# Cross-attention on one core: the loop's maxima are added onto the scores by accumulating transfers instead of GpSimd subtractions

## The chip, the cores and the metric

The kernel runs on one core of a Trainium2 chip. A core has TensorE (PE, matmuls; its weight loads are shown apart as PEld), VectorE (DVE), ScalarE (ACT), GpSimd (POOL) and SyncE (SP), and sixteen DMA engines that move data between HBM and the on-chip memory SBUF and within SBUF. The metric is the time of one execution on the device in microseconds.

## What is computed

For each of 16 batch items, 1024 query rows of 512 features attend to 64 context rows, in 16 heads of 32 features. Both inputs go through a layer norm whose scale and shift come from a condition vector. In the reference (cut to what matters):

```python
xq  = _ada_ln(x_q, t_vec, Wss_q, bss_q)
xkv = _ada_ln(x_kv, t_vec, Wss_kv, bss_kv)
q = (xq @ Wq + bq).reshape(B, Lq, nh, dh)
kv = (xkv @ Wkv + bkv).reshape(B, Lkv, 2, nh, dh)
scores = jnp.einsum('bqhd,bkhd->bhqk', q, k) / jnp.sqrt(jnp.float32(dh))
attn = jax.nn.softmax(scores, axis=-1)
out = jnp.einsum('bhqk,bkhd->bqhd', attn, v).reshape(B, Lq, H)
return x_q + (out @ Wp + bp)
```

All is float32. The change touches the softmax: the subtraction of the maximum of the scores ahead of the exponential.

## The kernel before the change

The queries are handled in 32 blocks of 512 rows (`NB = 32`). The engines' programs are written out by hand: the order of the calls in the Python text is the order in each engine's queue. A prologue computes keys and values for all batch items and starts the first blocks, a loop `for i in range(3, NB - 2)` (27 iterations) holds the steady state, and an end part finishes blocks 30 and 31. One iteration works on several blocks at once: the scores and the softmax of block `i`, the mix with the values and the output of `a = i - 1`, the rest of the output of `b = i - 2`, the query products of `n = i + 1`, the features of `f = i + 2`, and norm and transposes of later blocks.

The products of the queries and of the output use a scheme of seven products of half-size blocks (`query_product(n, k)`, `product(a, k)`), with sums of blocks made by GpSimd (`feature_sums`, `feature_quarters`, `row_sum`). Products add up in PSUM banks; `output_seed(a)` (L1039) is a ScalarE copy of one bank into another, onto which `product(a, 2)` then adds.

The softmax of block `i` goes this way. The 64 context rows are two halves, z = 0 and 1. `score_products(i, z)` (L738) makes the scores in PSUM, 32 keys of four heads on the partitions. VectorE takes the maximum of each 32 by transposing in the reduction (`maximum`, L755), ScalarE copies the scores to SBUF (`copied`, L764) as `s_tiles[i, z]`, 128 x 2048 values or 1 MB. `maxima(i)` joins the maxima of both halves on VectorE (L775, a tile `m` of 128 x 64) and spreads them back over the keys by a transpose (L784) into `mb`, again 128 x 2048. `subtract(i, zs)` (L797) subtracts `mb` from `s` in place, on GpSimd. `weights(i, z)` (L808) is ScalarE's exponential, in place for z = 0 and into a tile `p` for z = 1. Then `total(i)` adds both halves on GpSimd (L858), `swapped(i)` and `again` bring the halves into the form that the mix reads, and `row_total`, `inverse_rows` (L878, L881, L883, by way of a small tensor `ltd` in HBM and back as `vr`) and `spread_rows` (L891) make the inverse of the sums, by which `divided` (L915) multiplies the mix's results.

SyncE issues the transfers: loads of the block `x` (L119, 1 MB) and of the residual `r` (L126, 1 MB), the output (L1118, two halves of 512 KB), the moves `xt<-ht` (L382, sixteen of 64 KB for a block) that finish the transposition of the features, and the small ones of the inverse.

In the loop `subtract(i, zs=(0,))` and `subtract(i, zs=(1,))` are apart in the text, but no other GpSimd work lies between them. On ScalarE `weights(i, 0)`, `weights(i, 1)` and `output_seed(a)` follow one another, behind `scale_features(f, (3,))` (L442) and `biased(a, 2)` (L1031).

Of the kernel before, what the change touches and what calls it, by code (L numbers as in the profile page):

```python
# [11 lines left out]
ALU = mybir.AluOpType  # L12
# [8 lines left out]
def cross_attention_block(  # L21
# [18 lines left out]
    nc = tc.nc  # L40
# [10 lines left out]
    NB = B * BPB  # L51
# [675 lines left out]
    s_tiles, m_tiles = {}, {}  # L727
# [45 lines left out]
    def both(dst, src, op):  # L773

        nc.vector.tensor_reduce(dst, src.rearrange("p z r j -> p (r j) z"), AX.X, op)  # L775

    def spread(i, src, name, other=False):
        if other:

            t = qpool.tile([P, 4, NC, NT * 32], F32, tag="xt", name=name)  # L780
            t = t.rearrange("p g c n -> p (g c n)")
        else:
            t = rpool.tile([P, HPC * TB], F32, tag="spread", name=name)
        nc.vector.transpose(t, src.unsqueeze(2).to_broadcast([P, HPC * NJ, 32]))  # L784
        return t.rearrange("p (r q) -> p r q", r=HPC)

    mb_tiles = {}

    def maxima(i):

        m = small.tile([P, HPC * NJ], F32, tag="m", name=f"m_{i}", bufs=2)
        both(m, m_tiles.pop(i), ALU.max)
        mb_tiles[i] = spread(i, m, f"mb_{i}", other=i == NB - 1)

    def subtract(i, eng=nc.gpsimd, zs=(0, 1)):
        for z in zs:
            eng.tensor_tensor(s_tiles[i, z], s_tiles[i, z], mb_tiles[i], ALU.subtract)  # L797

    l_tiles = {}

# [548 lines left out]
    query_product(1, 6)  # L1349
    query_out(1, 6)  # L1350
    maxima(0)
    value_move("A", (3,))
    query_product(1, 7)
# [6 lines left out]
    value_move("A", (0,))  # L1360
    hidden(3, (0,))
    subtract(0, zs=(0,))
    q_stats(4, (0,))
    value_move("A", (1,))
    subtract(0, zs=(1,))
    q_stats(4, (1,))
    q_stats(4, (2,))
# [58 lines left out]
    feature_sums(2, nc.gpsimd, (1,))  # L1426
    maximum(1, 1, 1)
    maxima(1)
    context_out("B", "v", 4)
    context_out("B", "v", 5)  # L1430
# [18 lines left out]
    query_out(2, 2)  # L1449
    value_move("B", (2,))  # L1450
    subtract(1, zs=(0,))
    scale_features(3, (3,))
    context_product("B", "v", 3)
# [53 lines left out]
    maximum(2, 1, 1)  # L1507
    query_product(3, 6)
    maxima(2)
    row_total(1)  # L1510
    q_stats(6, (1,))
# [193 lines left out]
    y, z = NB - 2, NB - 1  # L1705
# [163 lines left out]
```

## Time and profile before

| | |
|---|---|
| median of 3 runs | 999.54 us (999.5 to 1000.05) |
| the profiled execution | 999.71 us |
| its span in the trace | 997.9 us |
| TensorE clock granted | full speed throughout |
| DMA | 165.77 MB, 166 GB/s in the mean |

The page gives the busy time of each engine, as a share of the span, and follows the chain of work that ended last back from the last instruction. A wait is put down to the instruction that ended it. "Landing" is the time from the issue of a transfer to its completion. Two rows of the page on DMA, in 40 slices of the span (tenths of the engines' time, and GB/s), show the level over the run:

```profile
DMA  9665736555655455466555554665555555444422
GB/s 314 233 195 149 191 90 178 152 164 182 188 177 175 154 176 150 148 187 188 180 176 150 175 158 141 187 187 181 173 153 174 147 155 183 147 136 133 142 81 97
```

### The profile page before, as it was taken

The numbers are of one execution on the slowest core, as the hardware profiler recorded it, in microseconds if no ns is written. First come the engines' busy times: TensorE is split into PE (matmuls) and PEld (weight loads), VectorE is DVE, ScalarE is ACT, GpSimd is POOL, SyncE is SP. The second block draws the span as 40 slices with busy tenths as digits, with TensorE's granted clock in tenths as the row PEclk, the third lists the DMA queues.
The fourth block names the chain that finished last, engine by engine and source line by source line (L and its number), as shares of the span: only waits on it lengthen the run. The fifth ranks groups of instructions, "written<-read, shape, count | busy, mean of one in ns | idle before, by whom it ended". The sixth has DMA issues, their size and how long they took to land.

```text
span 997.9 us, 20561 instructions
## 1 busy us (share of the span) xinstructions
PE 984.6 (99%) x7465; PEld 762.7 (76%) x7465; DVE 896.2 (90%) x1318; ACT 778.1 (78%) x1165; POOL 894.6 (90%) x690
## 2 busy tenths in 40 slices
PE   7999999999999999999999999999999999999997
PEld 7888777787777877877778778777787787777756
DVE  6787889999999999999999999999999999987786
ACT  3788778888888888888888888888888888876620
POOL 3668899999999999999999999999999999999681
PEclk9999999999999999999999999999999999999999
DMA  9665736555655455466555554665555555444422
GB/s 314 233 195 149 191 90 178 152 164 182 188 177 175 154 176 150 148 187 188 180 176 150 175 158 141 187 187 181 173 153 174 147 155 183 147 136 133 142 81 97
DMA packets 115188, 165.77 MB, mean 166 GB/s; under 512 B 34920, under 2 KB 46464, under 8 KB 113168
## 3 DMA queue, kind: packets, MB, share of 16 engines
q1 hardware_dynamic: 114704, 163.93, 55.3%
q8 instruction: 59, 0.97, 0.4%
q0 software_dynamic: 384, 0.54, 0.2%
q14 instruction: 41, 0.34, 0.1%
HBM read 79.47 MB, written 34.60 MB: 114 GB/s over the span
## 4 chain that ended last, share of the span: by engine, by line
PE 93%; DVE 3%; DMA 1%; issue 1%; SPq 0%; ACT 0%; DVEq 0%; ACTq 0%
PE pp L1086 36%; PE pq L534 30%; PE pq L605 10%; PE ps L738 7%; PE po L936 6%; PE pv_B L534 1%; PE pk_B L534 1%; PE pk_A L534 1%; PE pv_A L534 1%; DMA vr<-ltd 0%; DMA ltd<-lt 0%; DVE vb L891 0%; DVE m L755 0%; DVE xk_sums_A L493 0%; DVE l L826 0%
## 5 line engine op out<-in xcount | busy, mean ns | idle before, releaser
L797 POOL TENSOR_TENSOR s<-s,mb 128x2048 f32<-128x2048 f32 x64 | 290.6, 4563 | 20.3 <-DVE mb L784 12.3
L1086 PE MATMUL pp<-w_p_sb,ot 128*128 128x256 f32 x740 | 174.8, 380 | 1.2 <-DVE ot L915 1.2
L764 ACT COPY s<-ps 128x1024 f32<-128x1024 f32 x128 | 129.3, 1012 | 58.2 <-PE ps L738 46.5
L755 DVE TRANSPOSE_TENSOR_REDUCE m<-ps 128x32 f32<-128x1024 f32 x128 | 152.6, 1228 | 12.0 <-PE ps L738 11.5
L1086 PEld LDWEIGHTS pp<-w_p_sb,ot 128*128 128x128 f32 x740 | 138.6, 190 | 19.8 <-issue 1.8
L858 POOL TENSOR_TENSOR sum<-s,p 128x2048 f32<-128x2048 f32 x30 | 136.3, 4544 | 1.5 <-ACT p L808 1.5
L645 ACT ACTIVATE qt<-pq,bias_t 128x256 f32<-128x256 f32 x256 | 107.2, 471 | 34.2 <-PE pq L605 27.8
L1116 DVE TENSOR_TENSOR r<-pp,r 128x512 f32<-128x512 f32 x183 | 120.3, 669 | 13.6 <-ACT xt L442 5.8
L534 PE MATMUL pq<-xt,w_q_sums 128*128 128x256 f32 x512 | 123.8, 385 | 0.0
L534 PEld LDWEIGHTS pq<-xt,w_q_sums 128*128 128x128 f32 x512 | 95.1, 190 | 34.4 <-issue 22.6
L1086 PE MATMUL pp<-WT,ot 128*128 128x256 f32 x492 | 118.4, 384 | 0.0
L1086 PE MATMUL pp<-WT,s 128*128 128x256 f32 x488 | 116.1, 381 | 1.2 <-DVE r L1107 0.8
L817 ACT ACTIVATE s<-s 32x2048 f32<-32x2048 f32 x60 | 114.6, 1910 | 1.4
L1086 PEld LDWEIGHTS pp<-WT,ot 128*128 128x128 f32 x492 | 91.1, 190 | 18.3 <-issue 3.6
L327 ACT ACTIVATE x<-x,rstdq 128x512 f32<-128x512 f32 x128 | 94.8, 807 | 5.0 <-POOL rstdq L304 5.0
L1086 PEld LDWEIGHTS pp<-WT,s 128*128 128x128 f32 x488 | 88.3, 191 | 13.4 <-DVE r L1107 1.2
L442 ACT ACTIVATE xt<-xt,ss_q 128x512 f32<-128x512 f32 x124 | 94.4, 808 | 1.1 <-DMA xt<-ht 1.0
L915 DVE TENSOR_TENSOR ot<-po,vb 128x1024 f32<-128x1024 f32 x62 | 73.0, 1218 | 15.9 <-PE po L936 15.6
L493 POOL TENSOR_TENSOR xt_sums<-xt 128x512 f32<-128x512 f32 x64 | 81.2, 1268 | 6.2 <-ACT xt L442 6.0
L286 DVE BATCH_NORM_STATS2 bs<-x 128x6 f32<-128x512 f32 x128 | 85.3, 666 | 0.0
L891 DVE STREAM_TRANSPOSE vb<-vr 128x2048 f32<-128x2048 f32 (+1 forms) x33 | 73.8, 2238 | 6.2 <-DMA vr<-ltd 6.0
L357 DVE STREAM_TRANSPOSE ht<-x 128x512 f32<-128x512 f32 x124 | 77.5, 679 | 0.4 <-issue 0.2
(224 smaller groups left out, 1964.5 us busy)
## 6 DMA issues: line engine op xcount, KB each, us to landing
x<-in_x_dram SPq DMA_DIRECT2D x32, 1024.0 KB, 5.5
r<-in_x_dram SPq DMA_DIRECT2D x32, 1024.0 KB, 5.7
xt<-ht SPq DMA_DIRECT2D x488, 64.0 KB, 2.0
out_dram<-r SPq DMA_DIRECT2D x60, 512.0 KB, 4.8
p<-s SPq DMA_DIRECT2D x60, 256.0 KB, 3.8
wss_kv<-in_L_xcond_Wss_kv_dram SPq DMA_DIRECT2D x4, 512.0 KB, 7.2
wss_q<-in_L_xcond_Wss_q_dram SPq DMA_DIRECT2D x4, 512.0 KB, 11.6
vr<-ltd SPq DMA_DIRECT2D x128, 8.0 KB, 1.7
```

Source lines behind the costliest of these rows:

```text
L327: nc.scalar.activation(dst, src, AF.Identity, bias=rstd[:, 1, j : j + 1], scale=rstd[:, 0, j : j + 1])
L442: nc.scalar.activation(xt[:, :, c, :], xt[:, :, c, :], AF.Identity, scale=ss["q"][:, c, b : b + 1], bias=ss["q"][:, NC + c, b : b + 1],)
L534: nc.tensor.matmul(out_, lhsT=lhsT, rhs=rhs, start=new and m == 0 and c == 0, stop=c == HC - 1, skip_group_check=True,)
L605: nc.tensor.matmul(qa["q", k][:, q * P : (q + 1) * P], lhsT=lhsT, rhs=rhs, start=first and q == 0, stop=True, skip_group_check=True,)
L645: nc.scalar.activation(dst, src, AF.Identity, bias=bq_t[:, o : o + 1])
L755: nc.vector.tensor_reduce(m_tiles[i][:, z, 2 * e : 2 * e + 2, :], s_banks[i, z][e].rearrange("p r (j a) -> p r j a", a=32), AX.X, ALU.max, ...
L764: nc.scalar.copy(s_tiles[i, z][:, 2 * e : 2 * e + 2, :], s_banks[i, z][e])
L797: eng.tensor_tensor(s_tiles[i, z], s_tiles[i, z], mb_tiles[i], ALU.subtract)
L817: nc.scalar.activation(s_tiles[i, 0][at + 32 : at + 64], raw_tiles[i][at : at + 32], AF.Exp, scale=SCALE)
L858: nc.gpsimd.tensor_tensor(t, s_tiles[i, 0], s_tiles[i, 1], ALU.add)
L1086: nc.tensor.matmul(to, lhsT=rows[:, c, t * P : (t + 1) * P], rhs=cols[:, c, :], start=n == 2 and (i, 2) not in seeded and t == 0 and c == ...
L1116: nc.vector.tensor_add(r, a, r)
```

## The change

VectorE multiplies the joined maxima by -1 before they are spread, so `mb` holds the negative maxima, in all 32 blocks. In the 27 blocks of the loop `subtract` no longer runs on GpSimd's arithmetic: GpSimd issues a transfer from `mb` to `s_tiles[i, z]` with the accumulating operation add, one for each half, which adds `mb` onto what stands in `s`. In the blocks before and after the loop (0 to 2, 30 and 31) GpSimd adds `mb` where it subtracted before.

```diff
         m = small.tile([P, HPC * NJ], F32, tag="m", name=f"m_{i}", bufs=2)
         both(m, m_tiles.pop(i), ALU.max)
+        nc.vector.tensor_scalar_mul(m, m, -1.0)
         mb_tiles[i] = spread(i, m, f"mb_{i}", other=i == NB - 1)
 
-    def subtract(i, eng=nc.gpsimd, zs=(0, 1)):
+    def subtract(i, zs=(0, 1)):
+
         for z in zs:
-            eng.tensor_tensor(s_tiles[i, z], s_tiles[i, z], mb_tiles[i], ALU.subtract)
+            if 3 <= i < NB - 2:
+                nc.gpsimd.dma_start(s_tiles[i, z], mb_tiles[i], accum_op=ALU.add)
+            else:
+                nc.gpsimd.tensor_tensor(s_tiles[i, z], s_tiles[i, z], mb_tiles[i], ALU.add)
```

The lines behind the change move down by five (L808 becomes L813, L1039 becomes L1044). On GpSimd's queue, in one iteration of the loop (here block 9), the place of the two subtractions before; `t_quarters` is a work tile of the query products, `ot` the divided mix, `sum` the total of both halves:

```order
L581 TENSOR_TENSOR t_quarters<-xt_sums 128x256
L582 TENSOR_TENSOR t_quarters<-xt_sums,t_quarters 128x128
L583 TENSOR_TENSOR t_quarters<-xt_sums,t_quarters 128x128
L797 TENSOR_TENSOR s_0_3201<-s_0_3201,mb_3258 128x2048
L797 TENSOR_TENSOR s_1_3234<-s_1_3234,mb_3258 128x2048
L1051 TENSOR_TENSOR s_8_3342<-ot_3336 128x512
L1053 TENSOR_TENSOR ot_3336<-ot_3336 128x2x256
L858 TENSOR_TENSOR sum_3372<-s_0_3201,p_3359 128x2048
```

The same place in the changed kernel:

```order
L581 TENSOR_TENSOR t_quarters<-xt_sums 128x256
L582 TENSOR_TENSOR t_quarters<-xt_sums,t_quarters 128x128
L583 TENSOR_TENSOR t_quarters<-xt_sums,t_quarters 128x128
L800 DMA s_0_3210<-mb_3268 128x2048
L800 DMA s_1_3243<-mb_3268 128x2048
L1056 TENSOR_TENSOR s_8_3352<-ot_3346 128x512
L1058 TENSOR_TENSOR ot_3346<-ot_3346 128x2x256
L863 TENSOR_TENSOR sum_3382<-s_0_3210,p_3369 128x2048
```

Two arithmetic instructions have become two transfer issues at the same place; ScalarE's exponentials wait for the transfers' completion instead of for GpSimd.

On VectorE's queue, the place of the maxima in the same iteration before (`r` is the residual, `ps` the scores in PSUM, `pp` the output's bank):

```order
L1116 TENSOR_TENSOR r_2903<-pp_2_3077,r_2903 128x2x256
L755 TENSOR_REDUCE m_9_3200<-ps_1_1_3217 128x32
L755 TENSOR_REDUCE m_9_3200<-ps_1_0_3216 128x32
L775 TENSOR_REDUCE m_3256<-m_9_3200 128x64
L784 STREAM_TRANSPOSE mb_3258<-m_3256 128x2048
L1116 TENSOR_TENSOR r_2903<-pp_3_3140,r_2903 128x2x256
```

And in the changed kernel:

```order
L1121 TENSOR_TENSOR r_2911<-pp_2_3086,r_2911 128x2x256
L755 TENSOR_REDUCE m_9_3209<-ps_1_1_3226 128x32
L755 TENSOR_REDUCE m_9_3209<-ps_1_0_3225 128x32
L775 TENSOR_REDUCE m_3265<-m_9_3209 128x64
L793 TENSOR_SCALAR m_3265<-m_3265 128x64
L784 STREAM_TRANSPOSE mb_3268<-m_3265 128x2048
L1121 TENSOR_TENSOR r_2911<-pp_3_3149,r_2911 128x2x256
```

The row of L793 is new; the others stand as before, with the spread (L784) one place later.

## Prediction

> **What bounds the kernel now.** I read the page first: the span, the busy times and the chain that ended last. In the busy rows the first figure is us, then the share of the span, then the instructions.
>
> ```profile
> span 997.9 us, 20561 instructions
> PE 984.6 (99%) x7465; PEld 762.7 (76%) x7465; DVE 896.2 (90%) x1318; ACT 778.1 (78%) x1165; POOL 894.6 (90%) x690
> PE 93%; DVE 3%; DMA 1%; issue 1%; SPq 0%; ACT 0%; DVEq 0%; ACTq 0%
> ```
>
> TensorE is busy 99% of the span and carries 93% of the chain. Since a share of the span mixes prologue, loop and end, I then asked for windows of one loop iteration (from the first score product of one to that of the next). The columns are the window, its length, busy us of each engine with instructions, the granted clock, the DMA engines' busy share and GB/s.
>
> ```profile
> 408.67:437.19 28.52, 28.52 (x221) 22.17 (x221) 26.89 (x40) 24.14 (x35) 27.32 (x22) 1.00 0.57 166
> 437.19:465.70 28.51, 28.51 (x221) 22.17 (x220) 27.18 (x40) 23.94 (x35) 27.67 (x22) 1.00 0.58 172
> ```
>
> In the loop TensorE has no gap at all: 28.52 us busy of 28.52, at full clock. So whatever is taken off GpSimd (27.3 us of 28.5) can give back nothing in the loop: nothing waits for GpSimd that TensorE waits for. What counts is how little slack the steps around the change have before TensorE runs dry. I take the iteration from 408.67 us as the pattern of all 27; times below are in its trace.
>
> **What the change removes.** GpSimd's own row for the line, then its timeline where the two subtractions of one batch stand.
>
> ```profile
> L797 POOL TENSOR_TENSOR s<-s,mb 128x2048 f32<-128x2048 f32 x64 | 290.6, 4563 | 20.3 <-DVE mb L784 12.3 <-ACT qt L645 7.4 <-ACT s L764 0.4
> ```
>
> ```profile
> 418.33 0.45 POOL L583 TENSOR_TENSOR t_quarters<-xt_sums,t_quarters 128x128 f32<-128x128 f32 x1
> 419.08 9.06 POOL L797 TENSOR_TENSOR s<-s,mb 128x2048 f32<-128x2048 f32 x2 [0.30 <-ACT qt L645]
> 428.11 1.27 POOL L1051 TENSOR_TENSOR s<-ot 128x512 f32<-128x512 f32 x1
> 430.94 4.54 POOL L858 TENSOR_TENSOR sum<-s,p 128x2048 f32<-128x2048 f32 x1 [0.19 <-ACT p L808]
> ```
>
> 27 batches times 2 times 4.563 us is 246 us of GpSimd work gone; 10 of the 64 subtractions stay. Of this nothing reaches the end. The next GpSimd step is `row_sum(a, 0)` (L1051), which reads what VectorE divides at L915, and that is done only at 426.73 + 1.2 = 427.9 us (row below): GpSimd starts it at 428.1 now and could at 427.9. The one after the next, `total` at 430.94, waits for ScalarE's exponentials. So GpSimd would sit idle in the 9 us.
>
> **What the change puts on the path.** Here are the steps that the two results feed: ScalarE's exponentials (L808), its seed of a PSUM bank (L1039), and TensorE's products.
>
> ```profile
> 418.88 1.01 ACT L764 COPY s<-ps 128x1024 f32<-128x1024 f32 x1
> ...
> 425.60 0.82 ACT L442 ACTIVATE xt<-xt,ss_q 128x512 f32<-128x512 f32 x1
> 426.63 0.59 ACT L1031 COPY pp<-b_p_sb 128x512 f32<-128x512 f32 x1 [0.21 <-DVE r L1116]
> 427.16 1.91 ACT L808 ACTIVATE s<-s 128x2048 f32<-128x2048 f32 x1
> 428.97 1.90 ACT L808 ACTIVATE p<-s 128x2048 f32<-128x2048 f32 x1
> 430.77 0.58 ACT L1039 COPY pp<-pp 128x512 f32<-128x512 f32 x1
> ```
>
> ```profile
> 428.40 1.89 PE L1086 MATMUL pp<-w_p_sb,ot 128*128 128x256 f32 x8
> 430.12 1.89 PE L534 MATMUL pq<-xt_sums,w_q_sb 128*128 128x256 f32 x8
> 431.85 1.89 PE L1086 MATMUL pp<-w_p_sb,ot 128*128 128x256 f32 x8
> ```
>
> ```profile
> 431.64 1.70 PEld L1086 LDWEIGHTS pp<-w_p_sb,ot 128*128 128x128 f32 x8
> ```
>
> `product(a, 2)` (TensorE, 431.85; its weight load 431.64) accumulates onto the bank that `output_seed(a)` (L1039) fills, and that copy stands on ScalarE behind both exponentials. It ends at 430.77 + 0.58 = 431.35: **0.3 us before TensorE wants it**. The subtraction for z=1 ends at 419.08 + 9.06 = 428.14, the exponential on it starts at 428.97. So the second transfer must have landed by about 428.97 + 0.3 = 429.3, the first by 427.5; every microsecond later stops TensorE for a microsecond in every iteration, because the next batch's maxima hang on TensorE's own scores and so shift along.
>
> When can they start? VectorE's maxima and the spread:
>
> ```profile
> 416.30 0.29 DVE L775 TENSOR_REDUCE m<-m 128x64 f32<-128x128 f32 x1
> 416.62 2.31 DVE L784 STREAM_TRANSPOSE mb<-m 128x2048 f32<-128x2048 f32 x1
> 423.11 2.31 DVE L891 STREAM_TRANSPOSE vb<-vr 128x2048 f32<-128x2048 f32 x1 [0.41 <-DMA vr<-ltd]
> 426.73 2.36 DVE L915 TENSOR_TENSOR ot<-po,vb 128x1024 f32<-128x1024 f32 x2
> ```
>
> ```profile
> L216 DVE TENSOR_SCALAR early<-early 128x64 f32<-128x64 f32 x1 | 0.2, 198 | 2.5 <-ACT early L215 2.5
> ```
>
> The negation (128x64, same form and size as L216) is **0.2 us** on VectorE, 32 times, 6.3 us in all. It moves the end of the spread from 418.93 to 419.13. The work behind it on VectorE up to 423.11 has 0.41 us of idle time to take it up; without that cover it would cost up to 27 x 0.2 = 5.4 us. I take nothing for it, beyond the start of the first transfer at 419.3. The second is issued some 0.5 us later, when GpSimd's first issue is through and the last score copy (418.88 + 1.01) is done.
>
> How long does an accumulating megabyte take? The trace has none, so I bound it. From the answers on transfers: issue, count, KB each, median us from issue to landing; and GB/s in 40 slices of 418 to 434 us.
>
> ```profile
> x<-in_x_dram SPq DMA_DIRECT2D x1, 1024.0 KB, 5.3
> r<-in_x_dram SPq DMA_DIRECT2D x1, 1024.0 KB, 6.5
> xt<-ht SPq DMA_DIRECT2D x488, 64.0 KB, 2.0
> xt<-ht POOLq DMA_DIRECT2D x8, 64.0 KB, 2.5
> ```
>
> ```profile
> GB/s 69 0 41 8 12 1 0 0 19 20 16 7 159 56 113 138 46 143 41 159 56 128 353 328 343 148 210 333 399 410 410 410 410 405 374 241 123 143 184 323
> ```
>
> The plateau is 410 GB/s, so 1.049 MB is 2.56 us of the sixteen engines, and of the 5.3 us of a lone load 2.7 us are fixed. A transfer from GpSimd's queue lands 0.5 us later than the same from SyncE's. **Low bound**, one pass: each byte costs what a loaded byte costs. The first lands at 419.3 + 0.5 + 2.7 + 2.6 = 425.1, the second at 427.7: both in time, cost nothing. **High bound**, two passes (`mb` and the old `s` are both read for each byte written) with the other megabytes of that time going first: 2 x 2.56 = 5.1 us each, so 427.6 and 432.7; the residual load and the two halves of the output that SyncE issues at 424 to 427 us (rows below) are 2 MB or 5.1 us more: 437.8. I take two passes, since two operands have to be read where a load reads one, and for the sharing 1.2 us, the difference between the residual load (6.5 us, beside the output) and the lone load (5.3): the second lands at 433.9.
>
> [...]
>
> Sum: the exponential starts at 433.9 instead of 428.97, 4.9 us late; less the slack of 0.3 that is 4.6 us of stopped TensorE per iteration, and 27 x 4.6 = 124 us.
>
> **Transfers that the new ones meet.** SyncE's queue in the same stretch, with DMA engines' shares from windows (columns as above):
>
> ```profile
> 418.59 3.07 SPq L883 DMA_DIRECT2D vr<-ltd  x4
> 421.70 2.42 SPq L382 DMA_DIRECT2D xt<-ht  x4
> 424.16 0.58 SPq L126 DMA_DIRECT2D r<-in_x_dram  x1
> 426.03 0.98 SPq L1118 DMA_DIRECT2D out_dram<-r  x2
> ```
>
> ```profile
> 420.00:422.00 2.00, 2.00 (x14) 1.82 (x13) 1.90 (x7) 1.97 (x5) 2.00 (x1) 1.00 0.09 8
> 426.00:428.00 2.00, 2.00 (x23) 1.28 (x8) 1.87 (x3) 1.79 (x3) 2.00 (x1) 1.00 0.76 242
> 428.00:430.00 2.00, 2.00 (x11) 1.77 (x10) 2.00 (x3) 2.00 (x2) 1.92 (x3) 1.00 0.88 300
> ```
>
> The engines are nearly empty at 420 and 88% busy at 428, so the first transfer finds room and the second does not. Two small chains have almost no slack either: the last four quarter moves `xt<-ht` (last issue near 423.5, landing 2.0 us, so 425.5) are what ScalarE's L442 at 425.60 reads, and `vr<-ltd` already holds VectorE 0.41 us at 423.11. Each microsecond that the accumulations put on the moves delays ScalarE's L1031, which `product(a, 1)` needs at 428.4 (it ends at 427.2: 1.2 us of slack), and the exponentials behind it (0.5 us). With two passes this lies under the wait for the second transfer; with one pass it stands alone, bounded by 0 and by the whole 5.1 us of both accumulations going first, less 0.5: 27 x 4.6 = 124 us. Nearest row: the residual load's 1.2 us, of which 0.7 remain; 27 x 0.7 = 19 us.
>
> [...]
>
> **The rivals.**
> - **In time, no change** (also the case on the other side): an accumulating megabyte is one pass. It decides at 429.3 - (419.3 + 0.5 + 2.7) = 6.8 us for both, 3.4 us each. At 2.56 both land before they are read, and if the moves are not held up either the time is 999.7 us. For it: the bytes written are those of a load, and 420 to 426 us is nearly empty. Against: two reads. Chance 0.13.
> - **In time, but the moves are late**: one pass, with ScalarE and VectorE waiting 0.1 to 1.5 us per iteration for `xt` and `vr`: 1003 to 1040, from the row above 1019. Chance 0.20.
> - **Two passes** as summed: 1090 (no sharing: 432.7, so 3.8 - 0.3 = 3.5 us, 27 x 3.5 = 94) to 1160. Chance 0.42, the likeliest.
> - **DMA-bound**: the engines are busy 57% of 28.5 us = 16.3 us; 2 x 5.1 more is 26.5 us, 93%, so queues build up. Second landing at 437.8: 8.5 us, 27 x 8.5 = 230, 1229 us. Any slower adder goes beyond. Chance 0.15 up to 1230, 0.08 beyond.
> - **Faster**: fewer stalls through a free GpSimd or VectorE running undisturbed. TensorE has no gap in the loop to give; prologue and end keep their subtractions. Chance 0.02.
>
> **How the numbers follow.** The profiled execution took 999.71 us (span 997.9), beside a median of 999.54, so they are one; 999.7 + 124 is 1124. Low end: no change, 999. High end: the case in which everything else goes first, 1230. That leaves out about 0.1 above and a little below. Within 0.2%, about what a measurement of this kernel can tell from no change: 0.13; faster 0.02; slower 0.85.
>
> **What would show it.** Right: a loop iteration near 33 us; ScalarE's L808 waiting about 5 us for a DMA into `s`, then `product(a, 2)` waiting for L1039; the accumulations landing 9 us (first) and 13 to 14 us (second) after issue; GpSimd near 60% busy in the loop (27.3 - 9.1 + two issues of about 0.5, of 33); `xt<-ht` landing later than 2.0 us in that stretch. Wrong: both landing within 8 us; ScalarE waiting for `xt` or VectorE for `vr` instead; or GpSimd itself long at the issue, which would hold `row_sum` and with it the products 5 and 6.

## The result and the profile after

The changed kernel took **1227.97 us** (median, 1219.32 to 1232.68) against 999.52 us: 1.227 times as long, 95% interval 1.2239 to 1.2302. The forecast was 1124 us, slower; the time lies at the upper end of the range. The profiled execution has a span of 1230.2 us, 232.3 us more than before. The page's span and busy row:

```profile
span 1230.2 us, 20647 instructions
PE 1056.1 (86%) x7465; PEld 797.2 (65%) x7465; DVE 908.6 (74%) x1350; ACT 784.5 (64%) x1165; POOL 699.7 (57%) x690
```

GpSimd lost 195 us of work (246 us of subtractions, less 53 us of issuing) and TensorE, 99% busy before, is now at 86%. Two readings matter in the busy row: TensorE idles 174 us (1230.2 - 1056.1; before 13), and it is *busy* 71.5 us longer for the same 7465 matmuls. The list of waits (us in total, times, longest) has what the idle time waits for:

```profile
PE pp L1091 <- ACT pp L1036: 87.3, 26, 8.3
PE pp L1091 <- ACT pp L1044: 72.2, 19, 5.9
```

L1036 is the bias copy ahead of `product(a, 1)` (L1031 before), L1044 the seed ahead of `product(a, 2)` (L1039 before). 87.3 + 72.2 + 71.5 = 231 us: these three numbers are the loss. Behind the two stops stand two waits of ScalarE, for the moves `xt<-ht` and for the second accumulation:

```profile
ACT xt L442 <- DMA xt<-ht: 101.0, 21, 9.9
ACT p L813 <- DMA s<-mb: 70.8, 19, 5.4
```

Here the second is seen in one iteration, on ScalarE, then TensorE (start, us, engine, line, and in brackets the idle time before it):

```profile
504.25 0.81 ACT L442 ACTIVATE xt<-xt,ss_q 128x512 f32<-128x512 f32 x1 [2.20 <-issue]
504.98 0.58 ACT L1036 COPY pp<-b_p_sb 128x512 f32<-128x512 f32 x1
512.21 1.91 ACT L813 ACTIVATE p<-s 128x2048 f32<-128x2048 f32 x1 [4.82 <-DMA s<-mb]
514.03 0.58 ACT L1044 COPY pp<-pp 128x512 f32<-128x512 f32 x1
```

```profile
505.61 1.99 PE L1091 MATMUL pp<-w_p_sb,ot 128*128 128x256 f32 x8 [0.62 <-ACT pp L1036]
507.44 1.89 PE L534 MATMUL pq<-xt_sums,w_q_sb 128*128 128x256 f32 x8
514.66 3.78 PE L1091 MATMUL pp<-w_p_sb,ot 128*128 128x256 f32 x8 [5.33 <-ACT pp L1044]
518.24 2.89 PE L534 MATMUL pq<-xt,w_q_sums 128*128 128x256 f32 x8
```

The second exponential waits 4.8 us for the second accumulation, the seed behind it is late, TensorE stops for 5.3 us at the place that the prediction named. Then `product(a, 2)` takes 3.78 us where it took 1.89 before. Windows show why (window, length, busy us of PE, PEld, DVE, ACT, POOL, then the granted clock, DMA share, GB/s); the first row is the whole iteration:

```profile
485.09:522.78 37.69, 31.73 (x221) 24.05 (x220) 27.86 (x42) 24.30 (x35) 20.84 (x22) 0.91 0.72 185
507.40:509.30 1.90, 1.90 (x9) 1.34 (x8) 1.87 (x6) 0.00 (x0) 0.00 (x0) 1.00 1.07 151
514.60:516.50 1.90, 1.84 (x4) 1.52 (x5) 0.00 (x0) 1.90 (x4) 1.90 (x1) 0.50 1.05 406
516.50:518.30 1.80, 1.80 (x6) 1.41 (x5) 0.00 (x0) 0.26 (x1) 1.80 (x1) 0.50 0.58 225
518.30:521.00 2.70, 2.70 (x10) 2.24 (x9) 2.46 (x4) 1.60 (x6) 2.62 (x4) 0.64 0.52 109
```

After the stop the granted clock is 0.50 for 3.7 us and 0.64 in the mean of the next 2.7. Over the run the trace has 164 us at half clock, and TensorE is busy in 113 of them; that work would have taken half as long, so the clock accounts for about 57 of the 71.5 us (for the rest see e3).

Not all iterations are of this kind. In 8 of the 27 TensorE stops at `product(a, 1)` alone, as here (one row each of GpSimd, SyncE, ScalarE and TensorE):

```profile
644.49 1.79 POOL L800 DMA_DIRECT2D s<-mb  x2 [1.18 <-ACT s L764]
644.79 4.33 SPq L382 DMA_DIRECT2D xt<-ht  x4
657.29 0.81 ACT L442 ACTIVATE xt<-xt,ss_q 128x512 f32<-128x512 f32 x1 [6.99 <-DMA xt<-ht]
658.64 3.78 PE L1091 MATMUL pp<-w_p_sb,ot 128*128 128x256 f32 x8 [5.42 <-ACT pp L1036]
```

The last four moves are issued right behind the accumulations and land after up to 9.0 us instead of 2.0. ScalarE's feature scaling waits 7 us for them, and by the time its exponentials run, the second accumulation has landed. In the iteration shown first, three of the four were issued before the accumulations. The 8 iterations are exactly those in which all four moves come behind the first accumulation.

The transfers in the whole run (issue rows: count, KB, median us to landing; queue row: packets, MB, share of the sixteen engines' span):

```profile
s<-mb POOLq DMA_DIRECT2D x54, 1024.0 KB, 12.2
r<-in_x_dram SPq DMA_DIRECT2D x32, 1024.0 KB, 16.4
```

```profile
q0 software_dynamic: 8160, 57.16, 25.2%
```

GpSimd waits out the freed time: in the iteration shown first, where it issues the accumulations at 496.1, 6.5 us for VectorE ahead of L1056 and 7.1 us for ScalarE ahead of L863. GpSimd's queue held the engines 25.2% of 1230.2 = 310 us, 5.7 us for each of the 54 transfers. The residual load, 5.7 us before, now lands after 16.4.

### The profile page after: what moved, and what is told of

The parts are those of the page before. It is cut to its first block, busy times and chain, and to the rows that moved or that the text cites. A ratio compares the mean times of both kernels' runs of the same rounds, so it can differ in the third digit from the quotient of the medians.

```text
span 1230.2 us, 20647 instructions
## 1 busy us (share of the span) xinstructions
PE 1056.1 (86%) x7465; PEld 797.2 (65%) x7465; DVE 908.6 (74%) x1350; ACT 784.5 (64%) x1165; POOL 699.7 (57%) x690
## 3 DMA queue, kind: packets, MB, share of 16 engines
q0 software_dynamic: 8160, 57.16, 25.2%
## 4 chain that ended last, share of the span: by engine, by line
PE 37%; DMA 22%; issue 12%; DVE 11%; SPq 6%; POOL 6%; ACT 4%; ACTq 0%; POOLq 0%; DVEq 0%
PE pp L1091 16%; DMA s<-mb 15%; PE pq L534 11%; DVE m L755 4%; SPq L382 4%; DMA xt<-ht 4%; PE ps L738 3%; POOL sum L863 3%; ACT s L764 2%; PE pq L605 2%; DMA ltd<-lt 2%; SPq L888 1%; PE po L941 1%; DMA r<-in_x_dram 1%; DVE lt L868 1%
## 5 line engine op out<-in xcount | busy, mean ns | idle before, releaser
L1091 PE MATMUL pp<-w_p_sb,ot 128*128 128x256 f32 x740 | 220.1, 450 | 160.8 <-ACT pp L1036 87.3
L1091 PEld LDWEIGHTS pp<-w_p_sb,ot 128*128 128x128 f32 x740 | 158.4, 223 | 204.8 <-ACT pp L1036 97.7
L863 POOL TENSOR_TENSOR sum<-s,p 128x2048 f32<-128x2048 f32 x30 | 135.7, 4523 | 189.9 <-ACT p L813 183.1
L1056 POOL TENSOR_TENSOR s<-ot 128x512 f32<-128x512 f32 x30 | 38.0, 1267 | 187.5 <-DVE ot L920 187.5
L645 ACT ACTIVATE qt<-pq,bias_t 128x256 f32<-128x256 f32 x256 | 107.5, 473 | 40.1 <-PE pq L605 33.1
L534 PE MATMUL pq<-xt,w_q_sums 128*128 128x256 f32 x512 | 129.8, 398 | 0.0
L534 PEld LDWEIGHTS pq<-xt,w_q_sums 128*128 128x128 f32 x512 | 101.2, 202 | 37.8 <-issue 21.8
L813 ACT ACTIVATE p<-s 128x2048 f32<-128x2048 f32 x30 | 57.2, 1907 | 72.4 <-DMA s<-mb 70.8
## 6 DMA issues: line engine op xcount, KB each, us to landing
s<-mb POOLq DMA_DIRECT2D x54, 1024.0 KB, 12.2
r<-in_x_dram SPq DMA_DIRECT2D x32, 1024.0 KB, 16.4
```

The lines of the kernel that those rows point to most:

```text
L534: nc.tensor.matmul(out_, lhsT=lhsT, rhs=rhs, start=new and m == 0 and c == 0, stop=c == HC - 1, skip_group_check=True,)
L645: nc.scalar.activation(dst, src, AF.Identity, bias=bq_t[:, o : o + 1])
L863: nc.gpsimd.tensor_tensor(t, s_tiles[i, 0], s_tiles[i, 1], ALU.add)
L1091: nc.tensor.matmul(to, lhsT=rows[:, c, t * P : (t + 1) * P], rhs=cols[:, c, :], start=n == 2 and (i, 2) not in seeded and t == 0 and c == ...
```

## The experiments

My theory after the result: an accumulating megabyte is two passes of the DMA engines; so the second lands late, the feature moves beside them too, ScalarE's order of work passes both on to TensorE, and TensorE's clock adds to each long stop. Rivals: the negation; GpSimd's issue rather than the adding; the transfers' traffic slowing matmuls; and, of the two stops, that they add up.

| run | median us | ratio to before, 95% interval |
|---|---|---|
| e1 negation only | 1012.44 | 1.0106 to 1.0141 |
| e2 plain transfers | 1118.8 | 1.115 to 1.1221 |
| e3 one more exponential | 1037.99 | 1.0354 to 1.0401 |
| e4 three more | 1197.08 | 1.1939 to 1.1997 |
| e5 scaling later | 1235.76 | 1.2201 to 1.2513 |
| e6 seed first | 1322.53 | 1.3182 to 1.3267 |
| e7 both orders | 1206.5 | 1.2001 to 1.2127 |
| e8 residual early | 1200.43 | 1.1929 to 1.2079 |
| e9 one transfer | 1119.5 | 1.1126 to 1.1288 |
| e10 one transfer, scaling later | 1057.95 | 1.0527 to 1.0654 |
| e11 plain, scaling later | 1062.02 | 1.0601 to 1.0662 |
| e12 residual early, scaling later | 1204.68 | 1.2025 to 1.2095 |

**e1: the negation alone.**

```diff
-            if 3 <= i < NB - 2:
+            if False:
                 nc.gpsimd.dma_start(s_tiles[i, z], mb_tiles[i], accum_op=ALU.add)
```

> The negation stays on VectorE in all 32 blocks, but GpSimd adds the negative maxima everywhere; no accumulating transfer. Theory (the transfers are the whole loss): 999 to 1001 us, VectorE 6 us busier, TensorE still without a gap in the loop. Rival (the 0.2 us on VectorE pushes the spread or the quarter sums late in each iteration): 27 x 0.2 = 5 us or more, 1005 us.

12.6 us slower than before: both numbers were too low. The negation's row (min/median/max ns), then from the timeline GpSimd's work and one of them beside it, then TensorE's waits for VectorE's additions:

```profile
L793 DVE TENSOR_SCALAR m<-m x32: 194/788/1094, 72.5 to 966.5; 128x64 f32<-128x64 f32 x32
```

```profile
420.28 1.27 POOL L493 TENSOR_TENSOR xt_sums<-xt,xt_sums 128x512 f32<-128x512 f32 x1
420.81 0.79 DVE L793 TENSOR_SCALAR m<-m 128x64 f32<-128x64 f32 x1
```

```profile
PE pp L1091 <- DVE r L1121: 4.7, 25, 0.2
```

It takes 0.79 us, not the 0.20 of the row that I took its price from, and ends at 421.60, 0.05 us behind GpSimd's sum beside it (421.55). In the changed kernel's trace all 18 negations over 0.30 us end 0.05 us behind a GpSimd instruction that ran beside them; why, no run shows. The row of 0.20 us came from the prologue (at 3.5 us), where GpSimd had no arithmetic to do. VectorE, 94% busy in an iteration before, passes the delay on: TensorE now waits 0.2 us for its additions and an iteration takes 29.0 us instead of 28.5. In the changed kernel, with GpSimd idler, the median is 320 ns, in e2 and e9 about 700; what it costs there was not separated.

**e2: the same transfers without the adding.**

```diff
-                nc.gpsimd.dma_start(s_tiles[i, z], mb_tiles[i], accum_op=ALU.add)
+                nc.gpsimd.dma_start(s_tiles[i, z], mb_tiles[i])
```

> The same 54 transfers from GpSimd's queue, same bytes, same waits, without the accumulation: the negative maxima overwrite the scores, so the scores are left out of the exponential. Theory (an accumulating megabyte costs two passes, 5.7 us of the sixteen engines as the changed kernel's queue row gives it, a plain one half of that): transfers land 6 to 8 us after issue instead of 12.2, both stops shrink, 1000 to 1060 us. Rival (the cost is GpSimd's issue and its queue, not the adding): landing stays near 12 us and the time near 1228 us.

Its exponentials read the negative maxima in place of the scores. Its issue row, queue row, TensorE waits and ScalarE's wait for the moves:

```profile
s<-mb POOLq DMA_DIRECT2D x54, 1024.0 KB, 6.6
```

```profile
q0 software_dynamic: 8160, 57.16, 14.3%
```

```profile
PE pp L1091 <- ACT pp L1036: 62.0, 26, 4.0
PE pp L1091 <- ACT pp L1044: 5.6, 14, 0.4
ACT xt L442 <- DMA xt<-ht: 103.6, 27, 5.5
```

14.3% of 1114.6 us over 54 is 2.95 us of the engines for each, against 5.74: a ratio of **1.95**, for the same bytes written. Landing falls from 12.2 to 6.6 us, and the stop at the seed all but goes. So the adding is 109 us of the loss, and GpSimd's issue is not what delays: it fell too, from 0.98 to 0.55 us, but that is 0.4 us beside 5.6. But 119 us remain where I expected at most 60. The stop at `product(a, 1)` is 62 of them: ScalarE's first feature scaling waits for the moves there (one landed after 8.1 us). TensorE is also 44 us busier (1029.0 us), at most 26 of them by the clock (0.977 in the mean of 1114.6 us); the negation has a part too.

**e3 and e4: a late seed without any transfer.** The kernel of before; e3 has range(1), e4 range(3):

```diff
         weights(i, 1)
+        for _ in range(3):
+            nc.scalar.activation(s_tiles[i, 1], raw_tiles[i], AF.Exp, scale=SCALE)
         output_seed(a)
```

> The kernel of before, with the exponential of z=1 done twice ahead of the seed, so ScalarE brings the seed 1.8 us later and no transfer is touched. Both theories: TensorE stops 1.8 - 0.3 = 1.5 us in each of 27 iterations, 40 us, 1040 us; the stop is short and the granted clock stays at full speed.

> As the run with one more exponential, with three more: 5.4 us later, a stop of 5.1 us in each of 27 iterations. Theory (after a stop of that length TensorE runs at half clock for some us, as at 514 to 521 us of the changed kernel, 2.7 us lost per iteration): 27 x 7.8 = 210 us, 1210 us, TensorE busy about 70 us more than before, clock about 0.93. Rival (the extra TensorE time in the changed kernel comes from the transfers' traffic): 27 x 5.1 = 138 us, 1138 us, TensorE busy 985 us, clock 1.0.

The busy row and the wait of e3, then of e4:

```profile
PE 992.4 (96%) x7465; PEld 759.5 (73%) x7465; DVE 890.8 (86%) x1318; ACT 831.8 (80%) x1192; POOL 895.0 (86%) x690
PE pp L1086 <- ACT pp L1039: 30.7, 27, 2.3
```

```profile
PE 1053.6 (88%) x7465; PEld 805.6 (67%) x7465; DVE 893.7 (75%) x1318; ACT 934.0 (78%) x1246; POOL 895.8 (75%) x690
PE pp L1086 <- ACT pp L1039: 130.4, 27, 5.4
```

e3: 1038 us, as expected. The delay of 1.8 us costs 1.4 us an iteration, so the slack ahead of the seed is about the 0.3 us that the trace gave; the mean clock is 1.0. Yet TensorE is 7.8 us busier than before (992.4 against 984.6): about 0.3 us of each of its 27 stops counts as busy time with no change of the clock. e4: 1197 us; stops of 4.8 us (130.4 / 27), and TensorE is busy 69 us longer, 2.6 us per iteration, with not one transfer added; the mean clock of 0.942 over 1196.3 us stands for 69 us lost, stops included. So the stops are enough to explain it, and the rival (traffic slows the matmuls) falls. In the changed kernel, the 57 us of the clock and 0.3 us for each of the 45 stops make 70 of the 71.5.

Between the 1.1 us of e3's stops (30.7 / 27) and the 4.8 of e4's, the length alone does not settle it: in e2 a stop of 1.89 us was followed by a slow product (3.23 us), and one of 2.57 us by a product at full speed (1.99 us).

```profile
305.17 3.23 PE L1091 MATMUL pp<-w_p_sb,ot 128*128 128x256 f32 x8 [1.89 <-ACT pp L1036]
993.78 1.99 PE L1091 MATMUL pp<-w_p_sb,ot 128*128 128x256 f32 x8 [2.57 <-ACT pp L1036]
```

**e5, e6, e7: ScalarE's order.** In the changed kernel; e5 is the first edit, e6 the second, e7 both (there the scaling stands behind the exponentials):

```diff
-        scale_features(f, (3,))
         ...
         weights(i, 1)
         output_seed(a)
+        scale_features(f, (3,))
```

```diff
+        output_seed(a)
         weights(i, 0)
         query_product(n, 4)
         weights(i, 1)
-        output_seed(a)
```

> The changed kernel with the first feature scaling, which reads the moved features xt, put behind the seed on ScalarE, so that neither the bias copy ahead of product 1 nor the exponentials queue behind the moves. Theory (two waits in a row, but the second transfer lands late whatever ScalarE does before): the stop at product 1 (87 us) goes, the one at product 2 grows by most of it; 1190 to 1230 us. Rival (the two stops add, each with its own cause): 87 us and a third of the slow clock less, 1115 us.

> The changed kernel with the seed of the PSUM bank ahead of both exponentials on ScalarE, so product 2 no longer waits for the second transfer. Theory: its stop (72 us) and half of the slow clock (about 35 us) go, the stop at product 1 (87 us) stays: 1100 to 1140 us. Rival (late exponentials push ScalarE's next copies, and TensorE then stops at another product for as long): 1200 us or more.

> Both orders of ScalarE together: seed first, first feature scaling behind the exponentials. Theory: product 1 and product 2 wait for no transfer any more; what remains is ScalarE late behind the second transfer, with 4 us of idle time per iteration to take it up: 1000 to 1080 us, clock near 1.0. Rival (a DMA-bound loop: 16 us of old traffic and 11.5 of new per iteration): it cannot fall below about 27 x 1 us over 1000 and the moves hold ScalarE elsewhere: 1100 us or more.

The TensorE waits of e5; of e6 its two groups of products that wait (count, busy us, mean ns, idle us before them and for what) and ScalarE's wait for the moves; the TensorE waits of e7:

```profile
PE pp L1091 <- ACT pp L1044: 162.8, 27, 7.6
```

```profile
L1091 PE MATMUL pp<-w_p_sb,ot 128*128 128x256 f32 x740 | 225.5, 459 | 164.5 <-ACT pp L1036 163.5 <-DVE ot L920 0.9
L1091 PE MATMUL pp<-WT,ot 128*128 128x256 f32 x492 | 121.3, 389 | 37.8 <-ACT pp L1036 33.1 <-DVE r L1121 4.7
ACT xt L442 <- DMA xt<-ht: 156.0, 22, 9.1
```

```profile
PE pp L1091 <- ACT pp L1036: 106.7, 24, 6.4
```

e5: no faster, 1229 and 1242 us in its two runs, a little above what I expected. The stop at product 1 is gone and the one at product 2 is 162.8, all of 87 + 72. So the two stops do not add: without the moves ahead of it the second accumulation alone holds TensorE as long. e6: my theory fell, 1322 us. The stop at product 2 is gone, and the one at product 1 grows from 87 to 163.5 us, because ScalarE waits longer for the moves (156 us instead of 101): all four are issued behind the first accumulation in 22 of the 27 iterations, in the changed kernel in 8. So the moves too can hold TensorE for all of it. The rival's stop at another product is the smaller part: the seed waits for `product(a, 1)`, both exponentials come after it, and the next bias copy (L1036 a second time, ahead of product 7) is late, 33.1 us in 27 stops. e7: 1206 us, far above the 1080 I allowed. Its stop, too, is that next bias copy behind the exponentials, so the rival's number was right, but what the waits show is ScalarE's order (106.7 us for that copy); how full the DMA engines were is not shown for this run. No reordering that I tried hides the late landings.

**e8 and e12: the residual load out of the way.** e12 has e5's edit too.

```diff
+        load_residual(i)
         swapped(i)
         ...
         query_out(n, 3)
-        load_residual(i)
```

> The changed kernel with the residual load issued ahead of the swap on SyncE instead of behind the feature moves, so that it does not run beside the accumulating transfers. Theory (sharing with the residual load and the output is part of the second transfer's lateness): it lands 1 to 3 us earlier, 27 x 1 to 3 us and some slow clock less, 1130 to 1200 us. Rival (the accumulations are limited by themselves): no change, 1228 us.

> Both accumulating transfers, the residual load ahead of the swap, the first feature scaling behind the seed: only the second landing is left to wait for. Theory (the residual load shares the engines with it and costs it 1 to 2 us): the stop at product 2 falls from 163 us to 110 to 140 us, 1150 to 1195 us. Rival (the two transfers alone set it): 163 us and 1230 us as without the early load.

The TensorE waits of e8, then of e12:

```profile
PE pp L1091 <- ACT pp L1036: 113.6, 27, 8.3
PE pp L1091 <- ACT pp L1044: 23.3, 9, 4.4
```

```profile
PE pp L1091 <- ACT pp L1044: 85.6, 19, 5.6
PE pp L1091 <- DVE ot L920: 47.5, 9, 8.7
```

e8: 28 us less, the slow end of what I expected; with the load out of the way the accumulations land after 11.6 us in the median instead of 12.2 (at most 15.1 instead of 16.7), and the time falls by about 1 us an iteration. In e12 the stop behind the second accumulation falls from 163 (e5) to 86 us, more than expected, but the time only from 1236 to 1205: now the other chain without slack, `vr<-ltd` into VectorE's L920, holds TensorE 47 us. Why `vr` comes later there was not followed up.

**e9, e10, e11: one accumulation, or plain ones, and the moves out of the way.** In e9 only z=1 goes by transfer (`and z == 1`), and is issued ahead of GpSimd's addition for z=0; e10 adds e5's edit to e9, e11 adds it to e2.

```diff
-            if 3 <= i < NB - 2:
+            if 3 <= i < NB - 2 and z == 1:
         ...
+        subtract(i, zs=(1,))
         subtract(i, zs=(0,))
         ...
-        subtract(i, zs=(1,))
```

> One accumulating transfer instead of two: z=1 by transfer, issued first, z=0 added by GpSimd behind it. Theory (the second transfer's place in the queue makes the late landing): the one lands about 8 us after issue, in time, no stop at product 2; it takes as much engine time as two plain ones, so the feature moves are late as in the run with plain transfers: 1060 to 1120 us. Rival (any accumulating transfer lands late): a stop at product 2 remains, 1120 us or more.

> The run with one transfer, and the first feature scaling behind the seed on ScalarE. Theory (late moves behind the transfer are what is left): the stop at product 1 goes, what stays is the negation beside a busy GpSimd, 12 us: 1005 to 1030 us. Rival (the moves are needed as early by others): 1060 us or more.

> The run with plain transfers (scores left out of the exponential, since the negative maxima overwrite them), and the first feature scaling behind the seed. Theory (with one pass per megabyte both land in time, and only the feature moves cost): 1000 to 1030 us from 1119. Rival (the transfers' landing costs too): 1080 us or more.

e9's issue row, queue row and TensorE waits, then e11's waits of TensorE and VectorE:

```profile
s<-mb POOLq DMA_DIRECT2D x27, 1024.0 KB, 9.3
```

```profile
q0 software_dynamic: 4272, 28.85, 14.4%
```

```profile
PE pp L1091 <- ACT pp L1036: 56.8, 24, 3.6
PE pp L1091 <- ACT pp L1044: 5.2, 13, 0.4
```

```profile
PE pp L1091 <- DVE ot L920: 30.2, 15, 4.4
DVE vb L896 <- DMA vr<-ltd: 48.9, 18, 6.0
```

e9 is e2 again: one accumulation holds the engines 14.4% of the span, 5.9 us an iteration, as two plain transfers do, and the time is the same (1119.5 and 1118.8). It lands in time; what stops TensorE are the moves. With the scaling out of the moves' way e10 and e11 come down to 1058 and 1062 us, not to the 1030 I allowed: the small transfers of the inverse (`vr`) are the next to be late. No version beats the kernel of before.

## Why the prediction was right in kind and short in size

The direction and the mechanism came true; the size of 124 us came out as 228, and an iteration took 37.7 us (the one shown) where 33 was named. The case that was called the likeliest, 1090 to 1160 us, was missed, and the time fell at the upper edge of the range, which another case had set.

- **TensorE bounds the loop, GpSimd's freed time is worth nothing**: right. GpSimd idles 187.5 us ahead of L1056 for VectorE and 189.9 us ahead of L863, mostly for ScalarE.
- **0.3 us of slack between the seed and `product(a, 2)`**: right; e3 took 1.8 us and lost 1.4 an iteration.
- **Two passes**: right in price, 5.74 us against 2.95; that a second read is the reason, no run here shows.
- **Landing**: the first 8.0 us after issue, by the sum 8.3. The second stood at 512.1, 16.0 us after the first issue; the sum had 433.9 - 419.3 = 14.6. The short term was the price of each transfer (5.74 us against 5.1, so 1.2 us for both), or the sharing, for which 1.2 us were taken; a longer price can itself come from sharing, and no run separates them. The stop is 5.9 us on average (159.5 / 27) instead of 4.6.
- **The moves lie under the wait for the second transfer**: right in that the two stops do not add (e5), but the moves were taken too small. In 8 of 27 iterations they alone stop TensorE, and in e6 they cost it 163.5 us, as much as the second accumulation does in e5. So ScalarE waiting for `xt`, named as a sign of being wrong, came beside the sign of being right. With one pass they stand alone, as said, but at the far end of their bounds: 119 us in e2, clock and negation included, where I had 19 from the nearest row and 124 as the bound.
- **The sum's term that was missing**: every number was a wait; TensorE was taken to resume at full speed. The stops are long enough to drop its clock, and that is about 57 of the 228 us, most of the 71.5 that TensorE is busier. The sum "27 x 4.6" reads, as measured, 27 x (5.9 + 2.65) = 231.
- **The DMA-bound rival gave 1229 us**, close to the time, by another way: a second landing 18.5 us after the first issue and engines 93% busy. Seen were 16.0 us, and 72% over that iteration: its engine time per iteration, 26.5 us, was near (0.72 x 37.69 = 27.1), but the iteration grew with it. Its nearness is a coincidence of two errors.
- **The negation at nothing**: wrong by itself (12.6 us in e1). Its price came from a row with an idle neighbour, and its cover, 0.41 us of VectorE, was smaller than its real length.

Open: how much of the second landing's excess is sharing with the output, how much the queue; whether moves issued ahead of the accumulations would be in time; and the negation's part in the changed kernel.

## What to carry to other kernels

Taking work off an engine that the bounding engine does not wait for buys nothing, and replacing it by an accumulating transfer lengthens the way from operand to result: here 9 us of GpSimd for two halves became 16, at twice the DMA time of a copy (5.74 us against 2.95). Before moving work to the DMA engines, list the small transfers that share the stretch and their slack; those with 0.1 to 0.5 us were hit one after another. When a change stops TensorE for several microseconds, add the slow restart to each stop (here 2.65 us on top of 5.9). And when two late transfers lead to the same engine, as the moves and the second accumulation do here, taking one off the path buys nothing: the other holds it for as long (e5, e6).

## What the hardware showed that was not expected

- After the stop of 5.3 us above, the granted clock was 0.50 for 3.7 us and 0.64 in the next 2.7; with e4's stops of 4.8 us TensorE was busy 2.6 us longer for each (69 / 27), at a mean clock of 0.942; after stops of about 1 us (e3) the mean clock stayed at 1.0. In the changed kernel's trace from 160 us on, none of the 15 stops from 1.07 to 2.68 us had half clock within 1.5 us of its end, four of the six from 2.74 to 3.10 us had, and all 22 from 3.45 us up.
- A VectorE instruction of 0.20 us took 0.79 us beside a GpSimd sum and ended with it (e1).
- 64 KB moves that landed after 2.0 us in the kernel before took up to 9.0 us when two accumulating megabytes had been issued 0.3 us ahead of them (changed kernel, 644 us).
- An accumulating issue occupied GpSimd 0.98 us (changed kernel), a plain one of the same shape 0.55 (e2; medians).
